# First FFN of a macaron layer: its block list is cut from six batches instead of seven, and the seventh batch's row scatters move into the block stage

## The chip, the cores and the metric

The kernel runs on one core of a Trainium2 chip. The metric is device microseconds of one execution. The kernel before has a median of 1348.48 us over 9 runs (1335.18 to 1365.88). One execution was also taken with the hardware profiler.

Engines are named as the profile names them: PE (matrix products), PEld (loads of its stationary operand), DVE (vector), ACT (scalar), POOL (GpSimd, which also issues the indirect DMAs) and SP (which issues most plain DMAs; "SPq" is its DMA queue). L479 is line 479 of the kernel.

## What is computed

The input has 8 batches of 1024 tokens with 256 features. The layer is

```
x = x + 0.5 * ffn(layernorm(x))
x = x + linear_attention(layernorm(x))
x = x + 0.5 * ffn(layernorm(x))
```

Both FFNs have the same weights. Each has a shared expert, which all tokens pass, and 16 routed experts (256 to 128 to 256, gated by silu), of which every token passes two:

```
scores  = softmax(xf @ gate_w.T); two of four groups, then two of the experts left
h       = silu(xf @ We1.T + be1) * (xf @ We3.T + be3)
y       = sum over the two chosen experts of weight * (h @ We2.T + be2)
z       = silu(xf @ ws1 + bs1) * (xf @ ws3 + bs3) @ ws2 + bs2
result  = y + z
```

So 8192 tokens give 16384 rows of routed work in each FFN.

## The kernel before

**Routing by scatter.** `route` (L327 to L490) computes one batch's gate, picks the two experts of each token, and gives each of the 2048 rows a place in a DRAM buffer `xs_d`, in which every expert has a region. A running count per expert, `base`, goes from batch to batch. The generator yields after each step: gate products (gT), softmax (pr), group scores (gs), groups (cg), the first choice, the second choice with counts (sel, cum at L418 to L421), the ranks on PE (prk, L428), and the places (cw L445, rowi L461). With `fine` the sixth step is cut before the ranks. Then POOL writes the rows: for each of 4 groups an iota and a scaling (L468, L473), and four indirect DMAs of 128 rows (L479), 16 in a batch. With `fine` each scatter is a step, without it each group of four.

**Lists of blocks.** The block stage works on blocks of 256 rows. The first N1 blocks belong to one expert each; the blocks after them are made of two half blocks of 128 rows, which may belong to two experts. Two lists on one partition name, for each block or half block, the expert and the first row. The first list (`first_map` L556, through `listed` L510) counts only the whole blocks that a part of the batches already fills, so it can be made before the last batches are routed. The second (`second_map` L580) is cut when all rows are placed. Before, the first list takes seven of the eight batches in both FFNs: N1 = 40, and the second list holds up to 64 half blocks. The list operations on DVE run over 72 (NBH) places times 16 experts. 69 blocks (`USUAL`) run in any case. `fill_up` (L590) writes 17 blocks of zero rows behind the regions, on SP's queue.

**The stage ahead of the blocks (L1008 to L1030).** A loop over rounds r runs three things interleaved, a step each in turn: normalisation and transposition of batch r, routing of batch r-1, and the shared expert of batch r-2 (`shared_units` L845: `hidden` with p_s at L808, its silu on ACT at L812 and the gate product on DVE at L813; `outputs` with py_s at L827). In round 7 routing of batch 6 is run in one go ahead of the round's other work. In round 8 the first list is cut, two steps of batch 7's routing run, and the rest of it becomes `steps` for the block stage. The tiles of the normalised rows (tag "xn") rotate over 8 places, and list scratch and fill rows take places of the same ring.

**The block stage (`blocks` L624).** `biases` (L241) loads the experts' output biases `b2` (four DMAs of 512 KB, broadcast to the partitions). Then each iteration loads the rows of the block four ahead (`rows`: one DMA of 264 KB at L666 for a one-expert block, two of 132 KB at L672 for a two-expert block), copies the expert's weights (`weights` L684, DVE for the first expert, ACT for the second), transposes the next block (`transpose`: pxg on PE at L690, xgT on ACT at L695, the token places and weights `at` on DVE at L698 and L699, six places), multiplies the block (`first`: q on PE at L711, silu on ACT L717, product on DVE L718) and finishes the block two behind (`second`: qy on PE L737, bias copies b2c L735, a custom DVE operation with the weight L743, and two indirect scatters of 128 result rows to `ys_d` on POOL, L748). The order of instructions on every engine is the order of the code: the stage is under manual scheduling. After each iteration one step of `behind` (L606) is taken: seven steps of batch 7's routing, then in turn two of routing, one of the second list, one of the fills. So the steps end near block 34.

The first row load names the whole buffer `xs_d` and so waits for all scatters issued before it; the loads of the other one-expert blocks use a view of their own. The first two-expert load names the whole buffer again.

The attention between the FFNs uses the tag "ksb" (L925), which it shares with b2c, with 4 places. The second FFN's block stage is built by the same functions; it starts after attention and the second shared expert's work, and in it nothing of batch 6's rows is scattered late.

Of the kernel before, what the change touches and what calls it, by code (L numbers as in the profile page):

```python
# [10 lines left out]
F32 = mybir.dt.float32  # L11
# [4 lines left out]
ALU = mybir.AluOpType  # L16
# [3 lines left out]
P = 128  # L20
# [6 lines left out]
def macaron_kernel(  # L27
# [18 lines left out]
    nc = tc.nc  # L46
# [21 lines left out]
    VL = 8  # L68


    N1 = ((T - N) * K - E * (RB - 1)) // RB // VL * VL

    N2 = -(-((K * T - E) // P + E - NR * N1) // VL) * VL
    NBLK = N1 + N2 // NR
    NBH = -(-max(N1, N2 + 1) // VL) * VL
    MB = T // P


# [428 lines left out]
        nc.vector.tensor_reduce(nblk[:], more[:], axis=AX.X, op=ALU.add)  # L507
        return nblk

    def listed(nblk, off, name, res, unit):  # L510

        end = rp.tile([1, E], F32, tag="end", name=f"end_{name}")
        nc.vector.tensor_tensor_scan(end[:], ones[0:1, 0:E], nblk[:], 0.0, ALU.mult, ALU.add)
        after = half("xn", [1, NBH, E], f"after_{name}", BF16)
        nc.vector.tensor_tensor(
            after[:], iblk[0:1, :].unsqueeze(2).to_broadcast([1, NBH, E]),
            end[:].unsqueeze(1).to_broadcast([1, NBH, E]), ALU.is_ge,
        )
        lists = half("xn", [1, 3, NBH], f"lists_{name}")
        ev, rv, ok = (lists[:, i, :] for i in range(3))  # L520
        nc.vector.tensor_reduce(ev, after[:], axis=AX.X, op=ALU.add)
        yield


        step = nblk
        if off is not None:
            step = rp.tile([1, E], F32, tag="step", name=f"step_{name}")
            nc.vector.tensor_tensor(step[:], nblk[:], off[:], ALU.add)
            nc.vector.tensor_tensor(
                step[:, 0 : E - 1], step[:, 0 : E - 1], off[:, 1:E], ALU.subtract  # L530
            )
        nc.vector.tensor_tensor(
            after[:], after[:], step[:].unsqueeze(1).to_broadcast([1, NBH, E]), ALU.mult
        )
        nc.vector.tensor_reduce(rv, after[:], axis=AX.X, op=ALU.add)
        yield

        nc.vector.tensor_scalar(ok, ev, float(E), float(unit), ALU.is_lt, ALU.mult)
        nc.vector.tensor_tensor(rv, iblk[0:1, :], rv, ALU.subtract)
        if off is not None:  # L540
            nc.vector.tensor_tensor(
                rv, rv, off[:, 0:1].to_broadcast([1, NBH]), ALU.add
            )
        nc.vector.tensor_tensor(rv, rv, ok, ALU.mult)
        nc.vector.scalar_tensor_tensor(rv, ev, float(CAP), rv, ALU.mult, ALU.add)
        if off is not None:

            nc.vector.tensor_copy(rv[:, N2 : N2 + 1], end[:, E - 1 : E])
        rmap = rp.tile([1, NBH], I32, tag="rmap", name=f"rmap_{name}", bufs=2)
        nc.vector.tensor_copy(rmap[:], rv)  # L550
        nc.vector.tensor_scalar(ev, ev, float(E - 1), None, ALU.min)
        emap = rp.tile([1, NBH], I32, tag="emap", name=f"emap_{name}", bufs=2)
        nc.vector.tensor_copy(emap[:], ev)
        res.append((emap, rmap))
        yield

    def first_map(base, which):


        name = f"{which}a"  # L560
        cnt = counts(base, name, RB)
        nc.vector.tensor_scalar(cnt[:], cnt[:], -1.0, None, ALU.add)
        nblk = whole(cnt, name, ALU.is_ge)
        maps = []
        for _ in listed(nblk, None, name, maps, RB):
            pass
        end = rp.tile([1, E], F32, tag="done", name=f"done_{name}", bufs=2)
        nc.vector.tensor_tensor_scan(end[:], ones[0:1, 0:E], nblk[:], 0.0, ALU.mult, ALU.add)
        nc.vector.tensor_tensor(end[:], end[:], nblk[:], ALU.subtract)
        nc.vector.tensor_scalar(end[:], end[:], -1.0, float(N1), ALU.mult, ALU.add)  # L570
        nc.vector.tensor_scalar(end[:], end[:], 0.0, None, ALU.max)
        nc.vector.tensor_tensor(end[:], end[:], nblk[:], ALU.min)
        nc.vector.tensor_scalar(end[:], end[:], float(NR), None, ALU.mult)

        fill = half("xn", [P, DR], f"fill_{which}")
        nc.gpsimd.memset(fill[:], 0.0)
        nc.gpsimd.memset(fill[:, D : D + 1], float(SKIP))
        return maps, end, fill

    def second_map(base, which, maps, done):  # L580

        name = f"{which}b"
        last = rp.tile([1, E], I32, tag="last", name=f"last_{which}")
        nc.vector.tensor_copy(last[:], base[0:1, :])
        nblk = whole(counts(base, name, P), name, ALU.is_gt)
        nc.vector.tensor_tensor(nblk[:], nblk[:], done[:], ALU.subtract)
        yield last
        yield from listed(nblk, done, name, maps, P)

    def fill_up(last, fill):  # L590

# [11 lines left out]
            if e % 2:  # L603
                yield

    def behind(routing, base, which, maps, done, fill):  # L606

        for _ in range(7):
            next(routing)
            yield  # L610
        other = second_map(base, which, maps, done)
        last = next(other)
        yield
        fills = fill_up(last, fill)
        live = True
        while live:
            live = False
            for g in (routing, routing, other, fills):
                if next(g, StopIteration) is not StopIteration:
                    live = True  # L620
                    yield


    def blocks(maps, which, steps, between, tail):  # L624
# [7 lines left out]
        evals, rvals = {}, {}  # L632
        xg, wc, at, xgT, hh = {}, {}, {}, {}, {}
        b2 = biases(which)

        def values(i):

# [85 lines left out]
        def second(i):  # L723
            py = ps_y.tile([P, NR, D], F32, tag="y", name=f"qy_{which}_{i}")
            yo = mid.tile([P, NR, D], F32, tag="u3", name=f"yo_{which}_{i}", bufs=4)
            h, a = hh.pop(i), at.pop(i)
            w2s = [wall[:, bass.ds(e, 1), W2 : W2 + D] for e in evals[i]]
            b2c = []
            rest = mid.tile([P, NR], F32, tag="rest", name=f"rest_{which}_{i}", bufs=2)
            for s, e in enumerate(evals[i]):  # L730
                copy = nc.scalar.copy if s else nc.vector.tensor_copy
                b2c.append(
                    mid.tile([P, 1, D], F32, tag="ksb", name=f"b2c_{which}_{i}_{s}", bufs=4)
                )
                copy(b2c[s][:], b2[:, bass.ds(e, 1), :])  # L735
            for s in range(NR):
                nc.tensor.matmul(  # L737
                    py[:, s : s + 1, :], h[:, s * P : (s + 1) * P], w2s[s % len(w2s)],
                    start=True, stop=True,
                )  # L740
            for s in range(NR):

                nc.vector.tensor_tensor_reduce(  # L743
                    out=yo[:, s, :], in0=py[:, s, :], in1=b2c[s % len(w2s)][:, 0, :],
                    scale=a[:, s, 1:2], scalar=0.0, op0=ALU.add, op1=ALU.add,
                    accum_out=rest[:, s : s + 1],
                )
                nc.gpsimd.indirect_dma_start(  # L748
                    out=ys_views[i * NR + s][:, :],
                    out_offset=bass.IndirectOffsetOnAxis(  # L750
                        ap=a[:, s, 0:1].bitcast(I32), axis=0
                    ),
                    in_=yo[:, s, :], in_offset=None,
                    bounds_check=K * T - 1, oob_is_err=False,
                )
# [152 lines left out]
    def attention_q(b, xt):  # L908
# [12 lines left out]
        for c in range(NC):  # L921
            nc.tensor.matmul(
                pks[:, c * P : (c + 1) * P], ones[:], dg[:, c, :], start=True, stop=True
            )
        ksb = mid.tile([P, D], F32, tag="ksb", name=f"ksb_{b}", bufs=4)  # L925
        nc.scalar.copy(ksb[:], pks[:])
        pgt = ps_m.tile([P, NC, D], F32, tag="m", name=f"pgt_{b}")
        for ci in range(NC):
# [82 lines left out]
    for r in range(B + 1):  # L1011
        if r == 1:
            load_late_weights()
        if 2 <= r + 1 < B:
            xs[r + 1] = load_x(r + 1, x_v[r + 1])
        s = r - 2
        routing = None
        if r >= 1:
            routing = route(base, 0, r - 1, xns.pop(r - 1), xnTs[r - 1], r == B)
        if r == B:  # L1020
            maps, done, fill = first_map(base, 0)
            steps = behind(routing, base, 0, maps, done, fill)
        if r == B - 1:
            run(routing)
        run(
            normed(0, r) if r < B else None,
            routing if r < B else part(routing, 2),
            shared_units(xs[s], xnTs.pop(s), f"s0_{s}") if s >= 0 else None,
        )
        if 0 <= s < B - LATE:  # L1030
            nc.sync.dma_start(out=xk_d[s][:], in_=xs.pop(s)[:])
# [114 lines left out]
    def first_half():  # L1146
# [7 lines left out]
    ]  # L1154
    maps, done, fill, routing = last
    blocks(
        maps, 1, behind(routing, base, 1, maps, done, fill), by_block(moves), first_half
    )


# [133 lines left out]
```

## Time and profile before

| | |
|---|---|
| median of 9 runs | 1348.48 us (1335.18 to 1365.88) |
| profiled execution, its time | 1345.1 us |
| its span | 1343.4 us, mean granted clock 0.944 |
| stage ahead of the first blocks | 0 to 236 us, PE busy 192.72 |
| first block stage, one-expert blocks | 246 to 408 us |
| first block stage, two-expert blocks | 409 to 490 us |
| to the second block stage | 520 to 950 us, PE busy 400.20 |
| second block stage | 956 to 1240 us |
| row scatters L479 | 256, mean 1064 ns |
| result scatters L748 | 276, mean 997 ns |
| row loads | 80 of 264 KB, 116 of 132 KB |
| DMA over the span | 216.54 MB, mean 161 GB/s |

A line of a timeline gives the start in us, the duration (several instructions of one kind together), the engine, line, operation, output tile <- input tiles and the count; brackets give the idle time before it and what ended it. A line of waits gives the instruction that waited <- what it waited for: the total, the number of times, the longest. A line of groups gives count, busy us and mean ns, then the idle time before and its releasers. "remote" and "issue" stand for releases that the shown semaphores do not explain.

### The profile page before, as it was taken

The page shows a single profiled execution, that of the slowest core. Times are in us where ns is not written, and L with a number is a line of the kernel's source. Part 1 is how long each engine was busy: PE and PEld are TensorE (multiplying, and loading weights), DVE is VectorE, ACT ScalarE, POOL GpSimd, SP SyncE. Part 2 cuts the span into 40 slices and gives each one's busy share as a digit, 9 for nine tenths or more (in the row PEclk, how much of TensorE's full clock was granted, in tenths as well). Part 3 has the DMA queues.
Part 4 walks back from the last instruction along what each step waited for, and adds up shares of the span by engine and source line. Part 5 has one row for each costly group of instructions (what it writes and reads, how often), then busy time and mean ns, then how long its engine had stood idle before and what let it go on. Part 6 is the DMA issues. An engine that isn't in the chain of part 4 may idle for free. (4 is left out here: it accounts for less than half of the span.)

```text
span 1343.4 us, 20646 instructions
## 1 busy us (share of the span) xinstructions
PE 1171.4 (87%) x5728; PEld 850.2 (63%) x5728; DVE 892.9 (66%) x2878; ACT 539.0 (40%) x1119; POOL 592.7 (44%) x719
## 2 busy tenths in 40 slices
PE   6898787677888998899989899899878888988998
PEld 3454444566777885466666666575567768975565
DVE  6787557576455566876978768667476545654687
ACT  6556432222234552555666455434222224553110
POOL 1566556355665554000435564344156665555010
PEclk9999898788899999899999999899889989999999
DMA  9434322555666543623445321141445565542996
GB/s 353 152 127 155 117 108 86 174 171 171 207 184 174 159 147 108 220 94 126 158 158 200 150 92 57 49 158 54 155 154 168 172 187 161 158 136 92 338 366 252
DMA packets 96678, 216.54 MB, mean 161 GB/s; under 512 B 17446, under 2 KB 45355, under 8 KB 92465
## 3 DMA queue, kind: packets, MB, share of 16 engines
q1 hardware_dynamic: 68864, 139.11, 32.5%
q0 software_dynamic: 27696, 76.07, 15.3%
q8 instruction: 49, 0.80, 0.3%
q14 instruction: 69, 0.56, 0.1%
HBM read 115.09 MB, written 102.64 MB: 162 GB/s over the span
## 5 line engine op out<-in xcount | busy, mean ns | idle before, releaser
L748 POOL DMA_INDIRECT ys_d<-yo,at x276 | 275.2, 997 | 253.6 <-DVE rest L743 182.3
L711 PE MATMUL q<-xgT,wc 128*128 128x128 f32 (+1 forms) x1568 | 294.7, 339 | 69.9 <-ACT xgT L695 40.3
L479 POOL DMA_INDIRECT xs_d<-xn_f,rowi x256 | 272.3, 1064 | 113.4 <-issue 56.4
L711 PEld LDWEIGHTS q<-xgT,wc 128*128 128x128 f32 x1568 | 240.9, 203 | 96.8 <-ACT xgT L695 46.2
L695 ACT COPY xgT<-pxg 128x512 f32<-128x512 f32 x138 | 81.3, 589 | 286.8 <-PE pxg L690 122.6
L718 DVE SCALAR_TENSOR_TENSOR hb<-q,wc,hb 128x128 f32<-128x128 f32 (+1 forms) x196 | 73.6, 400 | 147.6 <-PE q L711 61.2
L808 PE MATMUL p_s<-xnT_f,ws_sb 128*128 128x512 f32 x352 | 163.4, 604 | 0.9 <-ACT hs_s L812 0.9
L743 DVE CUSTOM_DVE_ANT_0 yo<-qy,b2c,at 128x256 f32<-128x256 f32 x276 | 122.9, 482 | 56.2 <-remote 13.2
L827 PE MATMUL py_s<-ws_sb,hs_s 128*128 128x256 f32 x512 | 133.9, 406 | 24.8 <-DVE hs_s L813 18.6
L737 PE MATMUL qy<-wall,hb 128*128 x552 | 148.0, 392 | 2.7 <-DVE rest L743 2.7
L827 PEld LDWEIGHTS py_s<-ws_sb,hs_s 128*128 128x128 f32 x512 | 99.3, 201 | 63.2 <-DVE hs_s L813 30.9
L889 PE MATMUL pk<-wqk_sb,xnT_a 128*128 128x512 f32 x256 | 124.3, 603 | 0.1
L812 ACT ACTIVATE hs_s<-p_s,bc 128x512 f32<-128x512 f32 x64 | 43.7, 686 | 180.1 <-PE p_s L808 108.4
L737 PEld LDWEIGHTS qy<-wall,hb 128*128 128x128 f32 x552 | 104.5, 198 | 17.3 <-PE qy L737 2.5
L717 ACT ACTIVATE hb<-q,wc 128x128 f32<-128x128 f32 (+1 forms) x196 | 75.0, 418 | 85.0 <-PE q L711 39.1
L808 PEld LDWEIGHTS p_s<-xnT_f,ws_sb 128*128 128x128 f32 x352 | 66.7, 194 | 65.9 <-issue 62.3
L690 PE MATMUL pxg<-ident,xg 128*128 128x128 f32 x552 | 87.8, 285 | 15.5 <-DMA xg<-xs_d 15.5
L690 PEld LDWEIGHTS pxg<-ident,xg 128*128 128x128 f32 x552 | 73.0, 148 | 31.3 <-DMA xg<-xs_d 16.3
L473 POOL TENSOR_SCALAR xn_f<-cw 128x4 f32<-128x4 f32 x64 | 19.8, 315 | 146.6 <-DVE cw L445 108.6
L813 DVE SCALAR_TENSOR_TENSOR hs_s<-p_s,bc,hs_s 128x512 f32<-128x512 f32 x64 | 47.7, 747 | 48.3 <-PE p_s L808 31.9
L808 PE MATMUL p_s<-xnTr,ws_sb 128*128 128x512 f32 x160 | 70.4, 593 | 0.3 <-PEq L798 0.3
L897 PE MATMUL pgs<-xn_a,k 128*128 128x257 f32 x256 | 67.9, 388 | 0.8 <-ACT k L893 0.8
(302 smaller groups left out, 1709.3 us busy)
## 6 DMA issues: line engine op xcount, KB each, us to landing
xg<-xs_d SPq DMA_DIRECT2D x80, 264.0 KB
y<-ys_d SPq DMA_DIRECT2D x64, 256.0 KB
y<-ys_d SPq DMA_DIRECT2D x32, 512.0 KB
xg<-xs_d SPq DMA_DIRECT2D x116, 132.0 KB
xk<-x SPq DMA_DIRECT2D x8, 1024.0 KB
x<-xk SPq DMA_DIRECT2D x8, 1024.0 KB
wall<-in_wexp_dram SPq DMA_DIRECT2D x4, 1540.0 KB
x<-in_x_dram SPq DMA_DIRECT2D x6, 1024.0 KB
```

Of the source, the lines that this page charges most:

```text
L479: nc.gpsimd.indirect_dma_start(out=v[:, :], out_offset=bass.IndirectOffsetOnAxis(ap=rowi[:, j, k : k + 1], axis=0), in_=xn[:, t, :], in_of ...
L690: nc.tensor.transpose(pt[:, c, s * P : (s + 1) * P], xg[i][:, s, c * P : (c + 1) * P], ident[:],)
L695: nc.scalar.copy(xgT[i][:], pt[:])
L711: nc.tensor.matmul(pt_[:, cs], w[:, s, o + c * P : o + (c + 1) * P], t[:, c, cs], start=(c == 0), stop=(c == NC - 1),)
L717: nc.scalar.activation(h[:, cs], p1[:, cs], AF.Silu, bias=w[:, s, W2 - 2 : W2 - 1])
L718: nc.vector.scalar_tensor_tensor(h[:, cs], p3[:, cs], w[:, s, W2 - 1 : W2], h[:, cs], ALU.add, ALU.mult)
L737: nc.tensor.matmul(py[:, s : s + 1, :], h[:, s * P : (s + 1) * P], w2s[s % len(w2s)], start=True, stop=True,)
L743: nc.vector.tensor_tensor_reduce(out=yo[:, s, :], in0=py[:, s, :], in1=b2c[s % len(w2s)][:, 0, :], scale=a[:, s, 1:2], scalar=0.0, op0=ALU ...
L748: nc.gpsimd.indirect_dma_start(out=ys_views[i * NR + s][:, :], out_offset=bass.IndirectOffsetOnAxis(ap=a[:, s, 0:1].bitcast(I32), axis=0), ...
L808: nc.tensor.matmul(pt[:], w[:, c, s * P : (s + 1) * P], xnT[:, c, :], start=(c == 0), stop=(c == NC - 1),)
L827: nc.tensor.matmul(py[:, t - t0, :], hs[s][:, t * P : (t + 1) * P], ws2_sb[:, s, :], start=(s == 0), stop=(s == NS - 1),)
L889: nc.tensor.matmul(pk.rearrange("p k d -> p (k d)"), tile_of(axnT, c, j), wqk_sb[:, c, :], start=(c == 0), stop=(c == NC - 1),)
```

## The change

The numbers of the lists are now given per FFN. The first FFN's first list is cut from six batches (N1 = 32, up to 80 half blocks in the second list), the second FFN's from seven as before (40 and 64). With 80 half blocks the list operations of both FFNs run over 88 places instead of 72. In the first FFN blocks 32 to 39 thereby become two-expert blocks.

Routing of batch 5 is run in one go in round 6, and the first list is cut there, ahead of the round's other work. Routing of batch 6 gets the fine steps; its first eight (up to rowi) run interleaved in round 7, and its 16 row scatters, with their iotas and scalings, go to `behind` as `routed`: one in each of the first seven blocks, then one in each turn of five steps. `by` takes one step of `behind` in each of the first 8 iterations and two in each after that; the first seven of those take a scatter of batch 6 and a step of batch 7 each. The steps so end near block 26. The places of b2c and ksb go from 4 to 3.

```diff
+    LISTED = (B - 2, B - 1)
+    N1S = [(b * N * K - E * (RB - 1)) // RB // VL * VL for b in LISTED]
+    N2S = [-(-((K * T - E) // P + E - NR * n) // VL) * VL for n in N1S]
+    NBLK = max(n1 + n2 // NR for n1, n2 in zip(N1S, N2S))
+    NBH = -(-max(max(n1, n2 + 1) for n1, n2 in zip(N1S, N2S)) // VL) * VL
...
+    def by(gen, lead, n):
+        for _ in range(lead):
+            next(gen)
+            yield
+        live = True
+        while live:
+            for _ in range(n):
+                live = next(gen, StopIteration) is not StopIteration
+            if live:
+                yield
...
-    def behind(routing, base, which, maps, done, fill):
+    def behind(routed, routing, base, which, maps, done, fill):
         for _ in range(7):
+            next(routed, None)
             next(routing)
             yield
...
-            for g in (routing, routing, other, fills):
+            for g in (routed, routing, routing, other, fills):
...
-                    mid.tile([P, 1, D], F32, tag="ksb", name=f"b2c_{which}_{i}_{s}", bufs=4)
+                    mid.tile([P, 1, D], F32, tag="ksb", name=f"b2c_{which}_{i}_{s}", bufs=3)
...
-        ksb = mid.tile([P, D], F32, tag="ksb", name=f"ksb_{b}", bufs=4)
+        ksb = mid.tile([P, D], F32, tag="ksb", name=f"ksb_{b}", bufs=3)
...
-            routing = route(base, 0, r - 1, xns.pop(r - 1), xnTs[r - 1], r == B)
+            routing = route(base, 0, r - 1, xns.pop(r - 1), xnTs[r - 1], r > LISTED[0])
+        if r == LISTED[0]:
+            run(routing)
+            maps, done, fill = first_map(base, 0)
+        if r == B - 1:
+            routed, routing = routing, part(routing, 8)
         if r == B:
-            maps, done, fill = first_map(base, 0)
-            steps = behind(routing, base, 0, maps, done, fill)
-        if r == B - 1:
-            run(routing)
+            steps = by(behind(routed, routing, base, 0, maps, done, fill), 8, 2)
+            routing = part(routing, 2)
         run(
             normed(0, r) if r < B else None,
-            routing if r < B else part(routing, 2),
+            routing,
             shared_units(xs[s], xnTs.pop(s), f"s0_{s}") if s >= 0 else None,
         )
```

`listed` and `first_map` take N1S[which] and N2S[which] where they had N1 and N2; the second FFN calls `behind` with an empty `routed`.

More of the change, by code (lines that the diff above doesn't have):

```diff
@@ L68, in macaron_kernel @@
     VL = 8
[L71 to L75, printed above, removed]
+    LISTED = (B - 2, B - 1)
[3 more added lines that the diff above has]
+    NBH = -(-max(max(n1, n2 + 1) for n1, n2 in zip(N1S, N2S)) // VL) * VL
     MB = T // P
@@ L508, in whole, with listed @@
         return nblk
-    def listed(nblk, off, name, res, unit):
+    def listed(nblk, off, name, res, unit, n2):
         end = rp.tile([1, E], F32, tag="end", name=f"end_{name}")
@@ L546, in listed @@
         if off is not None:
-            nc.vector.tensor_copy(rv[:, N2 : N2 + 1], end[:, E - 1 : E])
+            nc.vector.tensor_copy(rv[:, n2 : n2 + 1], end[:, E - 1 : E])
         rmap = rp.tile([1, NBH], I32, tag="rmap", name=f"rmap_{name}", bufs=2)
@@ L564, in first_map @@
         maps = []
-        for _ in listed(nblk, None, name, maps, RB):
+        for _ in listed(nblk, None, name, maps, RB, None):
             pass
@@ L569, in first_map @@
         nc.vector.tensor_tensor(end[:], end[:], nblk[:], ALU.subtract)
-        nc.vector.tensor_scalar(end[:], end[:], -1.0, float(N1), ALU.mult, ALU.add)
+        nc.vector.tensor_scalar(end[:], end[:], -1.0, float(N1S[which]), ALU.mult, ALU.add)
         nc.vector.tensor_scalar(end[:], end[:], 0.0, None, ALU.max)
@@ L587, in second_map @@
         yield last
-        yield from listed(nblk, done, name, maps, P)
+        yield from listed(nblk, done, name, maps, P, N2S[which])
     def fill_up(last, fill):
@@ L634, in blocks @@
         b2 = biases(which)
+        N1, N2 = N1S[which], N2S[which]
         def values(i):
@@ L1156, in macaron_kernel @@
     blocks(
-        maps, 1, behind(routing, base, 1, maps, done, fill), by_block(moves), first_half
+        maps, 1, behind(iter(()), routing, base, 1, maps, done, fill), by_block(moves), first_half
     )
```

## The prediction

> **What bounds the kernel now.** I read the page's busy shares first, then the slices, the windows by stage, the timeline of TensorE and SyncE at the entry of each block stage, and last the waits and the queue of GpSimd inside the first block stage.
>
> ```profile
> PE 1171.4 (87%) x5728; PEld 850.2 (63%) x5728; DVE 892.9 (66%) x2878; ACT 539.0 (40%) x1119; POOL 592.7 (44%) x719
> PE   6898787677888998899989899899878888988998
> POOL 1566556355665554000435564344156665555010
> ```
>
> TensorE (PE) is the bound with 87%. The change adds nothing to its arithmetic: every row of q, qy and pxg is still multiplied once. So what can change is the 172 us in which PE is idle, and the half clock after an idle stretch. The low PE slices 7 to 12, counted from 0 (33.6 us each, 235 to 437 us), are the first block stage, where the change acts; POOL is some 50% busy there, not idle.
>
> The entry of the first block stage, PE and then SyncE (start, duration, line, tile; brackets give the idle time before and what ended it):
>
> ```profile
> 232.49 3.72 PE L827 MATMUL py_s<-ws_sb,hs_s 128*128 128x256 f32 x16 [1.20 <-DVE hs_s L813]
> 245.99 1.97 PE L690 MATMUL pxg<-ident,xg 128*128 128x128 f32 x8 [9.78 <-DMA xg<-xs_d]
> 247.78 3.78 PE L711 MATMUL q<-xgT,wc 128*128 128x256 f32 x8
> ```
>
> ```profile
> 231.37 1.77 SPq L248 DMA_DIRECT2D b<-in_be_dram  x4
> 243.23 18.21 SPq L666 DMA_DIRECT2D xg<-xs_d  x9
> ```
>
> ```profile
> 240.51 0.97 POOL L479 DMA_INDIRECT xs_d<-xn_f,rowi  x1 [0.30 <-issue]
> 258.54 1.00 POOL L748 DMA_INDIRECT ys_d<-yo,at  x1 [17.05 <-DVE rest L743]
> 263.01 0.98 POOL L748 DMA_INDIRECT ys_d<-yo,at  x1 [0.30 <-DVE mx_7b L308]
> 264.30 0.98 POOL L748 DMA_INDIRECT ys_d<-yo,at  x1 [0.30 <-DVE oh L316]
> ```
>
> PE stops at 236.2, batch 6's last scatter ends at 241.5, the first row load goes out at 243.2, and PE has its rows at 246.0: 9.78 us idle. The scatter is the named releaser. But the bias load (b, four DMAs of 512 KB) was issued at 231.4, and the window 236 to 246 shows a DMA share of 0.74. Whether the wait goes when the scatter does is told by the second FFN's entry, where no scatter stands ahead of the first load:
>
> ```profile
> 947.01 1.75 SPq L248 DMA_DIRECT2D b<-in_be_dram  x4
> 949.89 8.89 SPq L666 DMA_DIRECT2D xg<-xs_d  x6
> ```
>
> ```profile
> 956.46 1.97 PE L690 MATMUL pxg<-ident,xg 128*128 128x128 f32 x8 [5.73 <-DMA xg<-xs_d]
> ```
>
> There the same eight transposes still wait 5.73 us, with the DMA engines at 1.01 of their capacity from 951.0 to 956.4: the bias load shares the engines with the row loads. After it PE runs at a granted clock of 0.50 (956.4 to 960), as it does in the first FFN (246 to 250). So the half-clock piece stays.
>
> GpSimd (POOL) from 246 to 364, its groups (count, busy us and mean ns, idle before and its releasers):
>
> ```profile
> L748 POOL DMA_INDIRECT ys_d<-yo,at x50 | 50.0, 1000 | 55.2 <-DVE rest L743 38.3 <-issue 12.1 <-DVE b2c L735 2.2
> L479 POOL DMA_INDIRECT xs_d<-xn_f,rowi x11 | 11.2, 1019 | 4.0 <-issue 3.0 <-POOL xn_f L473 1.1
> ```
>
> And the waits of 260 to 405:
>
> ```profile
> ACT xgT L695 <- remote: 35.1, 5, 11.1
> PE q L711 <- ACT xgT L695: 17.2, 4, 7.1
> DVE at L698 <- DMA ys_d<-yo,at: 0.5, 1, 0.5
> ```
>
> PE's largest stalls here come through ScalarE's xgT copy, released by something outside the shown semaphores, and not through scatters. The last line is the lever by which POOL would reach PE: `at` has six places, so its copy of block i waits until the result scatters of block i-6 are issued and done.
>
> **The sum, part by part**, in us against the profiled execution (1345.1, span 1343.4, so 1.7 lie around the span).
>
> *Entry.* Removed: the first xg load's wait for batch 6's scatters. What is late next is the bias load and the xg load itself. By PE's idle time 9.78 - 5.73 = 4.05 are won; by the way from the bias load's issue to the first transpose (245.99 - 231.37 = 14.62 against 956.46 - 947.01 = 9.45) it is 5.2. The far end is all 9.8, if the rows came before the bias bytes. I take -4.5, because the second entry is the same code; ends -9.8 and -4.
>
> *Stage ahead of the blocks (0 to 236).* Routing of batch 5 now runs in one go a round earlier, batch 6 runs only its first eight steps beside the round, and the list is cut a round earlier. PE's work is the same. Removed from POOL here: 16 scatters, the 22.9 us from 218.6 to 241.5. Nothing but the entry waited for those. Moved on ACT: the places of the normalised rows rotate by one list's worth of tiles, so the normalisations of batches 6 and 7 (L282's mean 0.59 us, 16 of them 9.5) wait for batch 5's scatters and stand in ACT's queue ahead of gT and hs_s of the last rounds, for which PE waits. On the other side the list operations (1.33 us each at 222 to 231) leave the last round, where they cost an hs_s wait of 2.7 us on ACT (`hs_s L812 <- DVE lists_0a`), and batch 6's scatters no longer hold the tail. I follow the order of the queues by hand with the row durations and get an end some 3 us earlier: I take -3, ends -12 (all that the tail's waits of 200 to 236, 36.2 minus 27.6 busy, plus the list's 2.7, could give) and +10 (those 9.5 in front of PE, and 0.5 for a scatter wait).
>
> *Scatters in the blocks.* POOL from the first result scatter (258.54) to the 50th (ends 363.7) has 105.2 us. In it stand 61 scatters at a pitch of 1.285 (0.98 plus 0.30 issue) and three pairs of iota and scale of about 0.75: 80.6 us, so 24.6 idle. After the change there stand 50 result and 30 row scatters and seven pairs: 80 x 1.285 + 7 x 0.75 = 108.1 us. That is above the time there is, by 2.9. If none of the present idle time could be filled, it would be 19 x 1.285 + 4 x 0.75 = 27.4 late. The allowance: `at` of block i is written in iteration i-1, the scatters of block i-6 are issued in iteration i-4, so three pitches of 3.03 less the two scatters' 2.6, some 6.5 us. So the floor is 0 (2.9 is under the allowance), the ceiling 27.4 - 6.5 = 21. Idle time that waits on DVE's rest (38.3 in the row) is mostly waiting for PE's own stalls; a backlog fills it. I take +5, nearer the floor, ends 0 and +13 for the common case. Behind a late scatter on POOL stand the next yo (four places) and then DVE's custom operation and `at`, then PE's first matmuls.
>
> A rule speaks against this step. The Trainium skill, "SBUF — State Buffer", section "A bandwidth-pool intuition that's wrong", says that a DMA whose descriptors GpSimd writes, 620 ns alone, takes some 3100 ns beside a copying VectorE. No row here shows that lengthening: L479's scatters take 1029 ns from 60 to 236 and 1019 ns in the blocks, with VectorE 64% busy (76.4 of 120). By the page's figure, as an estimate, 80 scatters would need some 250 us instead of 108, and the sum would be +140; by the row nothing is added.
>
> *Blocks 32 to 39 become two-expert blocks.* PE's steady pitch is 3.03 for a one-expert block and 3.09 for a two-expert one: 8 x 0.06 = +0.5. With their stalls, 40 one-expert blocks take (408.57 - 247.78)/40 = 4.02 and 22 two-expert blocks 3.67: 8 x -0.35 = -2.8. ACT gains a weight copy (0.64) and a bias copy (0.42) in each, and is idle 118 of 159 us there (246 to 405). I take -1, ends -3 and +4. The new first two-expert load waits for all row scatters and fills, but those end at block 26 and it is needed at block 31 or so: 0, up to +4, held in the same ends.
>
> *Denser row scatters and fills beside the loads.* 17 fills of 132 KB now in some 18 blocks instead of 26; DMA share is 0.56 to 0.57 there: +1, ends 0 and +6 (one more stall of the size of the smaller ones, 5.46).
>
> *Three places for b2c and ksb.* ACT's bias copy then waits for the previous block's first reduction, which in the trace is done up to 0.5 earlier: 0, at most +0.4 in each of 30 blocks of which PE would see few.
>
> *Wider lists* (88 places for 72): 1.34 us operations become 1.64, four to a map, +1.2 per map. In the first FFN beside other work, in the second partly ahead of its entry: +1, ends 0 and +2.4.
>
> Sum: -4.5 - 3 + 5 - 1 + 1 + 0 + 1 = -1.5, so 1343.6 for an execution like the profiled one. The median of the nine runs shown is 3.4 above that one, so the median should be 1347.0.
>
> **Rivals.**
> 1. *POOL becomes the bound of the first 26 blocks* (slower). For it: 108.1 us of queue for 105.2. Against it: six places of `at`, and stalls of PE that a backlog uses. Price +21 for +5: 1363.0. It decides from the point where POOL is over 6.5 us behind; then `at` <- ys_d rows grow from 0.5 us to tens.
> 2. *ScalarE delays the last rounds ahead of the blocks* through the rotated places. For it: 16 normalisations ahead of gT and hs_s. Against: ACT is busy only 114 of 236 us, and may take them in its gaps. Price +10 for -3: 1360.0.
> 3. *Both the tail and the entry shorten fully* (faster). For it: all the waits of 200 to 246 end with routing or scatters. Against: the second entry's 5.73. Price -9.8 for -4.5 and -12 for -3: 1332.7.
> 4. *The wait is not removed at all*, some other scatter taking its place: batch 5's are issued a round earlier, batch 6's after the load in program order. I see no way; it would give 1351.5, within the middle.
>
> **How the numbers follow.** The likeliest case, 1347.0, is where the scatter wait is replaced by the bias load and the rest nearly cancels: 48%, with rival 4 in it; its own range is 1338 to 1357. Rival 1 has 20%, rival 2 14%, rival 3 18%. One per cent (13.5 us) is about what a measurement of this kernel can tell from no change: its runs go from 1335 to 1366. Rival 3 is all faster: 18%. Of rival 1 three quarters and of rival 2 half lie over 1362: 22%. The rest, 60%, is within. The range 1331 to 1364 leaves out the far half of rival 1 and what lies beyond rival 3.
>
> **What would show it.** Entry: the eight transposes' idle falls from 9.78 to about 5.7, released by xg, with the clock at 0.50 after it. Stage: py_s ends at 233 (224 to 246 by the ends). POOL: near 100% busy from block 0 to block 25, the 50th result scatter 3 to 10 us later measured from the first; `at` <- ys_d waits of a few us. Blocks 32 to 39: 128x128 q's, pitch near 3.7. I am wrong if the 9.78 shrinks below 4 (the bias load doesn't stand in the way), if `at` or yo waits sum to over 10 us, if stage one's end moves by more than 10, or if something changes by over 5 us after 520, where only wider lists and one less place differ.

## The result, and the profile after

The changed kernel takes 1367.29 us (median of 20 runs, 1356.04 to 1375.36), the kernel before 1349.0 (median of 62): a ratio of 1.0142, 95% interval 1.0122 to 1.0163. It is slower by 1.4%. The forecast was 1347.0 in a range of 1331 to 1364. On a second chip the same two gave 1.0111 (1.0069 to 1.0152).

The page of the changed kernel, its span and busy shares:

```profile
span 1367.5 us, 20852 instructions
PE 1165.4 (85%) x5792; PEld 844.5 (62%) x5792; DVE 897.7 (66%) x2886; ACT 547.3 (40%) x1142; POOL 604.6 (44%) x719
```

PE does no more work (1165 against 1171 us busy), so all of the 24.1 us by which the span grew is idle time of PE. Both traces, cut at the same points, show where (us; the points are the end of the last py_s, the first pxg, the first p_s behind the blocks):

| stretch | before | after | difference |
|---|---|---|---|
| stage ahead of the blocks, 0 to last py_s | 236.2 | 249.4 | +13.2 |
| entry, last py_s to first pxg | 9.8 | 5.9 | -3.9 |
| first block stage, first pxg to late p_s | 270.8 | 290.5 | +19.7 |
| the rest | 826.6 | 821.7 | -4.9 |

**The entry** did what was forecast. PE, SyncE and GpSimd there:

```profile
245.49 3.94 PE L844 MATMUL py_s<-ws_sb,hs_s 128*128 128x256 f32 x16
255.36 1.94 PE L707 MATMUL pxg<-ident,xg 128*128 128x128 f32 x8 [5.93 <-DMA xg<-xs_d]
```

```profile
245.73 2.12 SPq L250 DMA_DIRECT2D b<-in_be_dram  x4
249.20 8.67 SPq L683 DMA_DIRECT2D xg<-xs_d  x6
```

```profile
256.02 1.03 POOL L481 DMA_INDIRECT xs_d<-xn_f,rowi  x1 [15.12 <-DMA xg<-xs_d]
267.74 1.01 POOL L765 DMA_INDIRECT ys_d<-yo,at  x1 [9.41 <-DVE rest L760]
```

No scatter holds the first load any more, and the idle time is 5.93, as in the second FFN's entry before (5.73). The granted clock after it is 0.51 (255.4 to 259.0). The last fence shows a thing that was not foreseen: batch 6's first scatter waits 15.1 us, because now it writes `xs_d` behind the first load that names the whole buffer. GpSimd stands idle just ahead of the stretch in which it is short of time.

**The stage ahead of the blocks.** The waits of 200 to 530 (what waited <- for what: total, times, longest), and ACT's timeline:

```profile
ACT xn_f L284 <- DMA xs_d<-xn_f,rowi: 9.1, 1, 9.1
PE pg L346 <- ACT gT L342: 8.6, 1, 8.6
```

```profile
223.46 1.09 ACT L284 ACTIVATE xn_f<-x,nmr_f,rstd_f 128x256 f32<-128x256 f32 x2 [9.14 <-DMA xs_d<-xn_f,rowi]
224.46 0.35 ACT L342 COPY gT<-pgT 128x256 f32<-128x256 f32 x1
```

The normalisation of batch 7 waits on ACT for a place that batch 5's scatters still read; gT, which PE needs, stands behind it in ACT's queue, and PE waits 8.56. This is the mechanism that the prediction names as rival 2. Its reach is larger than that one wait: ACT normalises batches 6 and 7 from 127.4 and 158.4 us on in before, and from 204.5 and 210.5 on in the changed kernel.

Not all of the +13.2 can be laid to this. The gT of batch 4, before and after:

```profile
130.85 0.37 ACT L340 COPY gT<-pgT 128x256 f32<-128x256 f32 x1 [1.43 <-PE py_s L827]
141.19 0.37 ACT L342 COPY gT<-pgT 128x256 f32<-128x256 f32 x1 [2.61 <-PE py_s L844]
```

There the changed kernel is already 10.3 us behind, just after a wait of ACT of 10.89 us (up to 125.05) that is put down to "remote". In the changed kernel's second profile, on another chip, that wait is missing and the same gT starts at 128.65, ahead of before's. So one profiled pair can't tell how much of these 10.3 us is the change's. From this gT to the last py_s before takes 105.4 us and the changed kernel 108.2: 2.9 more.

**The blocks.** From the first result scatter (267.74) to the 50th (ends 395.8) GpSimd now takes 128.1 us against 105.2. Its groups from 255 to 396:

```profile
L765 POOL DMA_INDIRECT ys_d<-yo,at x50 | 53.1, 1063 | 36.6 <-DVE rest L760 22.8 <-issue 10.4 <-DVE wc L701 0.6
L481 POOL DMA_INDIRECT xs_d<-xn_f,rowi x32 | 32.9, 1027 | 28.6 <-DMA xg<-xs_d 15.1 <-issue 10.4 <-POOL xn_f L475 1.5
```

Of the 32 row scatters two lie ahead of the first result scatter, so 50 and 30, as counted. The second result scatters of blocks 5 to 14 are issued 4.3 to 11.4 us behind their data (scatter's start less end of rest); before, those of the same blocks 1.1 to 4.1. `at` waits for scatters only 3.8 us in all, and yo in no row of the same stretch. What these rows do not say is which of ACT's and PE's long waits come from GpSimd's lag (255 to 410):

```profile
ACT xgT L712 <- remote: 50.8, 6, 18.2
PE q L728 <- issue: 15.8, 2, 11.9
PE q L728 <- ACT xgT L712: 11.4, 3, 7.1
DVE at L715 <- DMA ys_d<-yo,at: 3.8, 2, 2.0
```

"Remote" waits stood in before's trace too (35.1 us in five in 260 to 405). Experiments had to tell what the moved scatters add to them.

### The profile page after: what moved, and what is told of

It is laid out like the page before. It is cut to its first block, busy times and chain, and to the rows that moved or that the text cites. A ratio compares the mean times of both kernels' runs of the same rounds, so it can differ in the third digit from the quotient of the medians.

```text
span 1367.5 us, 20852 instructions
## 1 busy us (share of the span) xinstructions
PE 1165.4 (85%) x5792; PEld 844.5 (62%) x5792; DVE 897.7 (66%) x2886; ACT 547.3 (40%) x1142; POOL 604.6 (44%) x719
## 5 line engine op out<-in xcount | busy, mean ns | idle before, releaser
L765 POOL DMA_INDIRECT ys_d<-yo,at x276 | 279.2, 1012 | 229.9 <-DVE rest L760 165.2
L728 PE MATMUL q<-xgT,wc 128*128 128x128 f32 (+1 forms) x1632 | 290.3, 329 | 84.4 <-ACT xgT L712 45.3
L481 POOL DMA_INDIRECT xs_d<-xn_f,rowi x256 | 278.6, 1088 | 130.4 <-issue 56.7
L735 DVE SCALAR_TENSOR_TENSOR hb<-q,wc,hb 128x128 f32<-128x128 f32 (+1 forms) x204 | 74.5, 392 | 160.7 <-ACT hb L734 66.5
L844 PE MATMUL py_s<-ws_sb,hs_s 128*128 128x256 f32 x512 | 133.4, 405 | 23.8 <-DVE hs_s L830 15.7
L475 POOL TENSOR_SCALAR xn_f<-cw 128x4 f32<-128x4 f32 x64 | 21.4, 339 | 166.9 <-DVE cw L447 129.0
```

The source lines that it names most:

```text
L481: nc.gpsimd.indirect_dma_start(out=v[:, :], out_offset=bass.IndirectOffsetOnAxis(ap=rowi[:, j, k : k + 1], axis=0), in_=xn[:, t, :], in_of ...
L728: nc.tensor.matmul(pt_[:, cs], w[:, s, o + c * P : o + (c + 1) * P], t[:, c, cs], start=(c == 0), stop=(c == NC - 1),)
L735: nc.vector.scalar_tensor_tensor(h[:, cs], p3[:, cs], w[:, s, W2 - 1 : W2], h[:, cs], ALU.add, ALU.mult)
L765: nc.gpsimd.indirect_dma_start(out=ys_views[i * NR + s][:, :], out_offset=bass.IndirectOffsetOnAxis(ap=a[:, s, 0:1].bitcast(I32), axis=0), ...
L844: nc.tensor.matmul(py[:, t - t0, :], hs[s][:, t * P : (t + 1) * P], ws2_sb[:, s, :], start=(s == 0), stop=(s == NS - 1),)
```

## Experiments

Each run's ratio is to the kernel before on the same chip. Chips differ: the kernel before takes 1324 us on that of the first four runs, 1327 on that of the next four, 1197 on that of the last three.

| run | ratio | 95% interval |
|---|---|---|
| scratch off the ring | 1.0070 | 1.0040 to 1.0099 |
| scatters ahead | 1.0128 | 1.0084 to 1.0172 |
| 32 blocks only | 1.0032 | 1.0003 to 1.0060 |
| dense steps | 1.0003 | 0.9972 to 1.0033 |
| changed kernel again | 1.0111 | 1.0069 to 1.0152 |
| both parts undone | 0.9995 | 0.9964 to 1.0026 |
| twelve at | 1.0039 | 1.0006 to 1.0072 |
| early burst | 0.9971 | 0.9935 to 1.0007 |
| early burst, late bias | 0.9840 | 0.9813 to 0.9866 |
| early burst, six at | 1.0023 | 1.0008 to 1.0038 |
| before with late bias | 0.9940 | 0.9922 to 0.9959 |

### The ring: scratch off the ring

```diff
-        more = half("xn", [1, E, MB], f"more_{name}")
+        more = half("k" if name == "0a" else "xn", [1, E, MB], f"more_{name}")
```

The same for `after`, `lists` and the first FFN's `fill`.

> The changed kernel, but the scratch of the first list and the fill rows take places of the tag k instead of places in the ring of the normalised rows. Theory 1 (rival 2 of the prediction: the rotated ring makes ACT's normalisation of batch 7 wait for batch 5's scatters, 9.1 us, and PE for gT behind it, 8.56 us): the stage ahead of the blocks ends near 236 to 241 instead of 249.4 and the median falls by 8 to 13, to 1354 to 1359. Theory 2 (routing of batch 5 in one go a round earlier, or the list on DVE, delays the round whatever the places): the stage ends at 247 to 250 and the median stays at 1364 to 1369.

Measured 1.0070, where 1.0142 and 1.0111 stand for the changed kernel: between a third and a half of the loss is gone. The wait of ACT for scatters is no longer among the waits, ACT normalises batches 6 and 7 from 126.5 and 157.5 on, as before, and the stage ends at 222.3 us. On one chip, the changed kernel's stage ends at 233.9 and that of the run with twelve `at`, which has the same edit, at 225.5: the ring costs 8.4. On the chip of this run, the stage of the kernel before ends at 229.1 (the run with dense steps, which leaves that stage as it was), so without the ring's wait it is 6.8 shorter than before, in one profile each. Theory 1 holds. What is left is in the blocks: 284.7 us from the first q to the late p_s.

### The scatters: scatters ahead

```diff
-            routed, routing = routing, part(routing, 8)
+            pass
...
-            steps = by(behind(routed, routing, base, 0, maps, done, fill), 8, 2)
+            steps = by(behind(iter(()), routing, base, 0, maps, done, fill), 20, 2)
```

> The changed kernel with batch 6's row scatters back ahead of the blocks, interleaved in round 7; the list is still cut from six batches, blocks 32 to 39 are still two-expert blocks. Block steps: one in each of the first 20 blocks, then two (all rows and fills are due before block 32's load). Theory 1 (in the blocks POOL is the bound, 80 scatters instead of 61 beside the first 25 blocks, some 20 us): the way from the first q to the late p_s falls from 288.7 to about 269, the entry wait returns (PE idle about 10 instead of 5.9), the median is 1349 to 1355. Theory 2 (the two-expert blocks or the wider lists cost the 20 us): that way stays over 283 and the median is 1366 to 1372.

The blocks' part came as theory 1 has it: 267.7 us from first q to late p_s, 17.0 less than the 284.7 of the run with the scatters moved on the same chip. The time was missed: 1.0128 instead of 1.000 to 1.005 (1349 to 1355 over 1349). The entry shows why:

```profile
231.65 3.94 PE L844 MATMUL py_s<-ws_sb,hs_s 128*128 128x256 f32 x16
257.08 1.94 PE L707 MATMUL pxg<-ident,xg 128*128 128x128 f32 x8 [21.49 <-DMA xg<-xs_d]
```

Interleaved in round 7 and not run ahead of it in one go, batch 6's scatters start at 229.8 and end at 252.5, so the entry waits 21.5 us and not 10. What is won in the blocks is paid at the entry.

### The two-expert blocks: 32 blocks only

The kernel before with `N1S`, `N2S` and NBH of the change (LISTED as there), three places for b2c and ksb, and `steps = by(behind(...), 20, 2)`; the list's counts still come from seven batches.

> The kernel before, its first list still cut from seven batches and batch 6's scatters ahead of the blocks, but only 32 one-expert blocks, 80 places for half blocks, lists 88 wide, three places for b2c and ksb; block steps one in each of 20 blocks, then two. Theory 1 (scatters and ring are the cost): 1346 to 1354, same as before. Theory 2 (two-expert blocks, wide lists and fewer places are the cost): 1360 to 1369.

1.0032 (1.0003 to 1.0060), 1329.5 us against 1324.1: theory 1. Eight two-expert blocks, wide lists and three places together cost 0 to 8 us. In the two profiles of the main comparison blocks 32 to 39 take 31.8 us (two experts) and 31.5 (one).

### The density of the steps: dense steps

```diff
-            steps = behind(routing, base, 0, maps, done, fill)
+            steps = by(behind(routing, base, 0, maps, done, fill), 8, 2)
```

> The kernel before with its own block steps taken denser: one in each of the first 8 blocks, then two, as the change does, but nothing of batch 6 among them. Theory 1 (number of scatters on POOL is the cost, 61 instead of 80 beside the first 25 blocks): POOL still has room, 1347 to 1353. Theory 2 (two steps in a block are the cost: two fills or list operations and scatters close together stall the loads, DVE and PE): 1356 to 1366.

1.0003 (0.9972 to 1.0033): two fills or list steps in a block cost nothing that is clear of the interval, some 4 us either way. Theory 1.

### The changed kernel again, and both parts undone

> The changed kernel once more, beside the next three, so that they have it on their chip. Measured before: ratio 1.0142 to the kernel before; on the other chip again 1.011 to 1.017.

1.0111, as expected.

Both edits above together ("k" for the scratch, batch 6's scatters ahead, steps 20 and 2):

> Both parts undone: scratch of the first list and fills in the tag k, and batch 6's scatters ahead of the blocks; list still from six batches, 32 one-expert blocks, block steps one in each of 20 blocks, then two. Theory 1 (ring and moved scatters are the whole cost): stage ahead of the blocks ends 5 to 10 earlier than with the ring as changed, the blocks take 266 to 268 from first q to late p_s, the entry wait is 10 again; ratio 0.998 to 1.005. Theory 2 (something else in the change costs too): 1.008 or more.

0.9995 (0.9964 to 1.0026). The blocks take 263.6 us, the stage ends at 227.5, and the entry waits 17.6, longer than the 10 expected, because batch 6's scatters end at 240.7 all the same. The blocks are 21.4 us shorter than in the changed kernel on the same chip (285.0), a second measure of the moved scatters beside the 17.0 above. Within the interval, some 4 us either way, ring and moved scatters are the whole cost; no third part of the change is needed to explain it.

### How GpSimd holds PE: twelve at

```diff
-            at[i] = mid.tile([P, NR, 2], F32, tag="at", name=f"at_{which}_{i}", bufs=6)
+            at[i] = mid.tile([P, NR, 2], F32, tag="at", name=f"at_{which}_{i}", bufs=12)
```

On top of the scratch off the ring.

> The changed kernel with the scratch in the tag k (ratio 1.007 without more) and twelve places for at instead of six. Theory 1 (GpSimd's backlog of 5 to 11 us reaches PE through the copy at of block i, which starts 3 to 4 us after the scatters of block i-6 were issued in blocks 11 to 18): with twelve places that wait is gone, the blocks' way from first q to late p_s falls from 284.7 to 268 to 274, ratio 0.992 to 0.999. Theory 2 (the four places of yo, or loads of code, fills and signals, hold PE, at only follows): 280 to 286, ratio 1.004 to 1.009.

A miss for theory 1: the blocks take 284.9 us, no less than with six places. The ratio (1.0039) lies at the edge of theory 2's range, and its interval (1.0006 to 1.0072) reaches into that range and not into theory 1's. `at` no longer waits for scatters: in blocks 15 and 20 it starts 3.9 and 3.3 us ahead of the issue of block i-6's scatters. But GpSimd's lag in block 10 grows to 15.8 us (11.0 in the changed kernel on the same chip), and the four places of yo stop DVE instead:

```profile
DVE yo L760 <- DMA ys_d<-yo,at: 11.5, 5, 4.1
```

More places move the wait from one tile to the next. They do not make GpSimd faster.

### Fewer scatters in the crowded part: early burst

```diff
-        for _ in range(7):
-            next(routed, None)
+        for k in range(7):
+            for _ in range(4 if k < 2 else 1):
+                next(routed, None)
```

On top of the twelve places.

> As the one with twelve places of at, and of batch 6's scatters four in each of the first two blocks, before the first result scatter, where GpSimd is idle for 9.4 us; then one in a block. Theory 1 (the number of scatters beside the result scatters sets the time): six fewer scatters of 1.285 in the crowded part, 3 to 8 us below the run with twelve places alone, ratio 0.988 to 0.997. Theory 2 (another bound): same as that run within 3 us.

0.9971 (0.9935 to 1.0007): 11.4 us below the run without the burst (1322.06 against 1333.5), more than the 3 to 8 expected. The blocks take 270.6 instead of 284.9. Six scatters more in GpSimd's idle time, and PE gains over ten. So the number of scatters beside the result scatters counts. The six alone are 7.7 us (6 x 1.285); the intervals of the two runs don't tell 11.4 from that.

### The same with six at

> The changed kernel with the scratch in the tag k and the early burst, but six places for at as before. Theory 1 (the number of scatters in the crowded part is what counts, the places only decide who waits for GpSimd): same as with twelve places within 3 us, ratio 0.995 to 1.000, blocks from first q to late p_s 268 to 275. Theory 2 (the six places of at cost by themselves, 1.007 against 1.0039): 1.001 to 1.005, blocks 276 to 283.

Measured 1.0023 (1.0008 to 1.0038), blocks 242.1. This was on the chip where the kernel before takes 1197 us, so the blocks' 268 to 283 can't be applied. The ratio lies in theory 2's range, but with no run of twelve places alone on that chip it doesn't settle what the six places cost. The run gave something else. On that chip no wait is put down to "remote", in any of the three runs, and GpSimd's part can be seen by itself. Blocks 8 to 23, the windows of this run and, behind it, of the kernel before with the late bias (length, then busy us of PE, PEld, DVE, ACT, POOL; granted clock, DMA share, GB/s):

```profile
233.70:301.00 67.30, 55.50 (x258) 42.09 (x257) 43.88 (x161) 16.97 (x32) 52.68 (x56) 0.97 0.67 211
```

```profile
247.00:298.60 51.60, 50.07 (x259) 42.08 (x258) 41.79 (x160) 16.96 (x32) 39.65 (x42) 1.00 0.72 222
```

GpSimd's groups in the same stretches:

```profile
L766 POOL DMA_INDIRECT ys_d<-yo,at x29 | 32.3, 1114 | 8.8 <-issue 3.0 <-DVE b2c L753 2.1 <-DVE rest L761 0.9
L481 POOL DMA_INDIRECT xs_d<-xn_f,rowi x17 | 17.1, 1004 | 5.5 <-issue 3.4 <-POOL xn_f L475 1.8 <-DMA xs_d<-xn_f,rowi 0.3
```

```profile
L748 POOL DMA_INDIRECT ys_d<-yo,at x30 | 30.3, 1011 | 11.3 <-DVE rest L743 4.0 <-issue 3.4 <-DVE b2c L735 1.5
L479 POOL DMA_INDIRECT xs_d<-xn_f,rowi x8 | 9.6, 1204 | 2.9 <-issue 1.5 <-DMA xg<-xs_d 0.6 <-POOL xn_f L473 0.5
```

With 46 scatters the 16 blocks take 67.3 us; 46 gaps of 0.30 are 13.8, and with 52.7 busy that is 66.5: GpSimd has nothing left. PE has 11.8 us idle in it. With 38 scatters they take 51.6 us, PE is busy for 50.1 of them, 3.2 us a block. GpSimd is the bound in the one and PE in the other; the DMA engines are not fuller where it is slower (0.67 against 0.72). And here the waits (200 to 340) name the path, `at` for the scatters of six blocks before:

```profile
DVE at L716 <- DMA ys_d<-yo,at: 18.6, 9, 3.4
```

Without batch 6's scatters in the blocks it is 4.2 us in three (195 to 340).

The two kernels also differ in the list, the density of the steps and the place of the bias load, so this pair by itself does not show that all of the 15.7 us between them are the scatters'.

### The bias load behind the row loads

```diff
-        b2 = biases(which)
+        b2 = []
...
                 rows(i)
+            if lo == 0:
+                b2.append(biases(which))
             weights(lo)
```

`second` reads b2[0]. Once on top of the early burst with twelve `at`:

> As the run with the early burst (ratio 0.9971), but the bias load (four DMAs of 512 KB) is issued behind the first four row loads instead of ahead of them, in both FFNs. Theory 1 (the prediction's: what is late next at the entry is the bias load, which waits for PE's last p_s and shares the DMA engines): the rows are there when PE ends the stage, the entry's idle of 6.4 and the second entry's 5.6 fall below 2.5 each, GpSimd's first scatter of batch 6 no longer waits 18 us for the first row load; ratio 0.987 to 0.993. Theory 2 (the bias load itself is needed by then, or the list and its registers hold the loads): the entries stay at 5 or more, ratio 0.995 to 0.999.

Measured 0.9840 (0.9813 to 0.9866), better than expected, and faster than the kernel before; the changed kernel itself was not run on this chip. Its first entry:

```profile
191.30 3.94 PE L847 MATMUL py_s<-ws_sb,hs_s 128*128 128x256 f32 x16
195.08 1.04 PE L708 MATMUL pxg<-ident,xg 128*128 128x128 f32 x8
196.91 1.97 PE L729 MATMUL q<-xgT,wc 128*128 128x256 f32 x8 [0.79 <-ACT xgT L713]
```

PE goes on without a gap, and at full clock (8 q in 1.97 us, against 3.78 at before's entry). GpSimd's wait for the first load is 5.1, against 14.5 in the run with six `at` on the same chip and 18.3 in the early burst on another. In the blocks GpSimd still holds PE, now through yo and then qy:

```profile
DVE yo L761 <- DMA ys_d<-yo,at: 29.5, 13, 4.0
PE qy L755 <- DVE rest L761: 13.9, 7, 2.2
```

And once on the kernel before:

> The kernel before with the bias load behind the first four row loads, in both FFNs; batch 6's scatters stay ahead of the first load. Theory 1 (bias load is second in the first FFN, first in the second FFN): the first entry's wait for the scatters stays and ends 1 to 4 earlier without the bias beside the rows, the second entry's 5.6 falls below 2.5; ratio 0.994 to 0.998. Theory 2 (the bias is needed itself): 0.999 to 1.002.

Measured 0.9940 (0.9922 to 0.9959). The second entry's gap is gone:

```profile
850.32 3.94 PE L829 MATMUL py_s<-ws_sb,hs_s 128*128 128x256 f32 x16
854.09 1.04 PE L690 MATMUL pxg<-ident,xg 128*128 128x128 f32 x8
```

The first entry still waits 18.9 us there, for batch 6's scatters. So the bias load stood in the way at both entries. With batch 6 in the blocks the first one is won too: 0.984 against 0.994, of which the two kernels' other differences are also part.

## Why the prediction was wrong, step by step

**Entry: right.** -4.5 was taken, -3.9 measured, from the second FFN's entry as the nearest row. That the bias load is late next is shown by moving it. The far end, all of the idle time "if the rows came before the bias bytes", is what the run with the late bias then reached.

**Stage ahead of the blocks: wrong, the first failed step.** -3 was taken, and the profiled pair shows +13.2. Of that 10.3 is there by batch 4's gT, behind a "remote" wait that the second profile of the changed kernel doesn't have, so +2.9 is the part that the pair lays to the rounds behind it. The step that failed is the rotated places: the mechanism was named (rival 2), but the value taken puts it at about nothing (ACT "may take them in its gaps"), and even the far end has only "0.5 for a scatter wait". That wait is 9.1, PE waits 8.56 behind it, and on one chip the ring costs 8.4. The other half of the step was right: without the ring's wait the stage is shorter, by 6.8 against the 3 taken. Rival 4 has batch 5's scatters "issued a round earlier". They are not: from batch 4's gT to the first of them it is 60.3 us, before 60.8. Their scaling waits 7.57 us for DVE's cw until 197.5, the 16 go out from 201.5 to 227.7, and three of them take 2.0 to 3.0 us instead of 0.97.

**Scatters in the blocks: wrong in size, the second failed step and the larger.** +5 was taken of 0 to 21; 17.0 and 21.4 were measured between two runs each on two chips. The count was right (50 and 30, 108.1 us of queue). The step that failed is "a backlog fills it". GpSimd took 128.1 us for queue work of 108.1: 20 us of idle time and longer scatters stayed. With 24.6 us of idle before, nearly all of rival 1's price of 21 came.

How GpSimd holds PE is named by the waits of other runs: on the last chip `at` (18.6 us) or, with twelve places, yo (29.5) waits for scatters, and on the second yo (11.5). In the changed kernel's own profile the prediction's sign for it, "`at` or yo waits sum to over 10 us", did not come (3.8), though the cost did. That there too DVE stops when GpSimd lags, and GpSimd waits for PE again when the lag is worked off, so that the two follow one another, is argued and not shown.

**Two-expert blocks, density, three places, wider lists: right** within the runs' intervals (1.0032 and 1.0003 for their parts, against -1, +1, 0 and +1 us).

**The rest.** That both rivals could come at once was given no case of its own: the cases were drawn as alternatives, and both prices together (1347.0 + 16 + 13 = 1376) lie outside each of them. The terms that the runs give, -3.9 for the entry, +2.9 for the rounds and 17 to 21 in the blocks, come to 16 to 20 us; the medians differ by 18.3 here and by 15.6 on the second chip. The profiled pair differs by 24.1; the -4.9 behind the blocks is of the size by which a kernel's profiled execution and its median differ here (3.4 for the kernel before) and has no cause shown.

**The rule weighed there.** The page "SBUF — State Buffer" of the Trainium skill, section "A bandwidth-pool intuition that's wrong", would have a scatter wait beside a copying VectorE, some 3100 ns instead of 620. The scatters of the crowded part take 1063 and 1027 ns in the mean, so the loss came in the main from their number. But "No row here shows that lengthening" was read from means, and single scatters show it. One of batch 5's, with the list operation that runs beside it:

```profile
207.88 1.60 DVE L534 TENSOR_TENSOR after_0a<-after_0a,nb_0a 1x1408 bf16<-1x1408 bf16 x1
208.00 2.33 POOL L481 DMA_INDIRECT xs_d<-xn_f,rowi  x1 [0.30 <-DMA xs_d<-xn_f,rowi]
```

It takes 2.33 us instead of 0.97 and ends 0.85 us after VectorE's operation on two tensors (210.33 against 209.48); the one at 204.41, beside a comparison up to 205.57, does the same (2.01 us, 0.85 after). The one at 206.72 begins in a reduction of 1.61 us and takes its 0.97. Four of batch 5's scatters are lengthened, by 4.9 us together, three of them beside operations of the list, which the change puts there; all four end before ACT's wait of 9.1 us does (223.46). In the crowded part five take 1.6 to 2.4 us, 4.3 us together more than 0.98 each, of the 20 us that stayed.

**Open.** What "remote" is was not found. In the traces of the other chips ACT and DVE wait for signals of PE up to 17 us after the matmuls' ends (pxg of block 18 of the changed kernel ends at 325.0, its copy starts at 341.6), at places that shift with the program. The moved scatters cost 17.0 and 21.4 us on chips that show such waits, and two runs with and without them differ by 15.7 us in 16 blocks on the chip that shows none, so a cost of this size does not need them.

## What to carry to other kernels

Work moved off a stage's entry must be weighed in the queue that it moves to: count the issues per block times the pitch there, and where the sum passes what PE takes for a block, take the whole excess and do not let idle time that was measured under another bound pay for it. When an allocation is moved in a rotating set of places, look for whose readers now stand ahead of each new writer, and for what else waits in that writer's queue. Before a stage's difference in one profiled pair is laid to the change, look where in the stage it arises, and whether a second profile has it. When a wait is taken away, the next one behind it (a bias load of 2 MB) was here cheaper to move than the first.

## What was not expected of the hardware

The kernel before has medians of 1349, 1324, 1327 and 1197 us in runs on different chips; its granted clock is 0.944 in the first's profile and 0.981 to 0.986 in the runs on the last. Why is not shown. On the last no wait is put down to "remote" in the three runs profiled there; the kernel before has 88.7 us of it on ACT's xgT alone on the first:

```profile
ACT xgT L695 <- remote: 88.7, 13, 11.3
```

The parts of a sum are read more cleanly on the chip without such waits.
